# Masked self-attention on one core: rows and values turned by transposing transfers, scores of two heads and two blocks per run on 64-row tiles

## The chip, the cores and the metric

The kernel runs on one core of one Trainium2 chip. The metric is device time in microseconds (us) of the whole program, the median of several runs; beside it stands one profiled execution of the same program, with its own span.

The core's engines are named as in the profile: PE multiplies matrices (PEld is its loading of weights), ACT applies functions such as the exponential, DVE does element-wise work, POOL and SP mostly issue transfers (POOLq and SPq are their queues). SBUF is the on-chip memory of 128 rows (partitions); PSUM is the memory of 8 banks that PE writes, each 512 f32 columns wide.

## The reference, cut to what matters

```python
# x: (16, 512, 1024) f32; mask: (16, 1024) of 0 and 1; Wq, Wo: (512, 512)
xt = jnp.transpose(x, (0, 2, 1))                      # B, T, D
q = xt @ Wq.T
qh = q.reshape(B, T, 8, 64).transpose(0, 2, 1, 3)
scores = 0.125 * jnp.einsum('bhqd,bhkd->bhqk', qh, qh)
logits = (scores * cmask + (1.0 - cmask) * -1e30) * rmask
attn = jax.nn.softmax(logits, axis=-1)
ctx = jnp.einsum('bhqk,bhkd->bhqd', attn, qh)         # values are the queries
out = ctx.transpose(0, 2, 1, 3).reshape(B, T, D) @ Wo.T
return x + jnp.transpose(out, (0, 2, 1))
```

Queries, keys and values are one projection, so scores are symmetric. A token whose mask is 1 attends to all tokens whose mask is 1. A token whose mask is 0 has equal logits and gets the plain mean of all values.

## The kernel before

About half of a batch's 1024 tokens are active. For each of the 16 batches (a loop index `b`) the kernel gathers the active rows to the front, pads to a width `A` of 544 columns (5 batches), 528 (9) or 512 (2), and does the attention on these alone; the other rows get one projected mean added. Above 512 columns, the last 32 or 16 tokens are "the tail" and have their own small tiles.

The steps for a batch, by function:

- `index`, `gather`: a one-hot product finds the rows; POOL moves them in by indirect transfers, four tiles `xa` of 128 x 512 and one tail tile `xt`.
- `xt`: turns each tile on PE (four f32 transposes, L486) into columns; `xsplit` (L444, L445) copies them from PSUM as a sum of two f16 parts, `xh` on ACT and `xl` on DVE.
- `query`: `q` = Wq x, in eight accumulations (four 128-row groups `e`, each two heads; two column halves `g`) of 12 products (L513): weight high x input high, high x low, low x high.
- `qsplit`: DVE splits `q` into f16 parts; four copies on SP's queue (L540 to L543) build `xx`, which puts a head's high part on 64 rows and its low or high part on the other 64. A product over all 128 rows then gives two of the score terms at once.
- `value`: turns the queries back into rows on PE (L569) and copies them (L572); the squares' row maxima (`squares`, `peaks`, `top`, `bottom`) give the shift `nm` of each head's exponentials. `value_tail` does the same for the tail.
- `scores`: for head `p` and block `i` of 128 tokens, four products (two terms, two column halves, L701) into two of PSUM's banks, then one exponential on ACT with its row sum (L705). There are two such pairs of banks. With `i` None it does the tail tokens of four heads on 32-row outputs (L676).
- `attend`: sums over blocks, values as weights, on 64-column tiles of PE for the two heads of a pair, in f32 (L726); the tail's part on 128 rows (L730); the sums are copied by ACT (L734).
- `recip_sums`, `recip_rows`: reciprocals of the row sums, turned on PE (L764), written to memory and read back as broadcast rows `rb` (L769, L773). Four times a batch, once per pair of heads.
- `norm`: multiplies (L799), mixes in the mean for padding (L800) and splits into f16 `ch`, `cl`.
- `project`: twelve 512-wide products per 128 tokens (L817), added to the gathered row (L822) and scattered by POOL (L901). `project_tail` does the tails of three batches together. `rest` adds the mean to inactive rows (L888).

`run` lays out 18 steps a batch: one step per pair of heads and block, and two for the tails. Beside each step's two runs of scores it hands out other work of the batch before (its norms and projections) and of the next (turns, queries, values) by the planned costs in a list `m`. The final order on PE is the scheduler's, with priorities (`high_priority`) and edges (`issue_after`) where the text asks for them. A shift above `MMAX` raises a flag that lets a slow general path run after all.

Of the kernel before, what the change touches and what calls it, by code (L numbers as in the profile page):

```python
# [32 lines left out]
CQ = C + 2  # L33
# [3 lines left out]
MMAX = 60.0  # L37
# [9 lines left out]
class Fast:  # L47
# [12 lines left out]
    def __init__(self, ctx, tc, x, x_nat, mask_t, wq_t, wo_t, out):  # L60
# [9 lines left out]
        self.ps_s = pool("ps_s", 2, space=PS)  # L70
        self.ps_av = pool("ps_av", 1, space=PS)
        self.ps_m = pool("ps_m", 2, space=PS)
        self.st = {}
        self.group_first = None
# [14 lines left out]
    def pm(self, shape):  # L89
        return self.ps_m.tile(shape, F32, tag="m", name="pm")  # L90


    def setup(self, mask_t):
# [42 lines left out]
        self.qt = fixed("qt", [P, 2, HG, CT])  # L136
        self.number = iota("number", [P, B - 2], [[1, B - 2]], 2, 0)

    def setup2(self):
# [4 lines left out]
        self.xh = fixed("xh", [P, DC, CQ], F16)  # L144
        self.xl = fixed("xl", [P, DC, CQ], F16)
        for t in (self.xh, self.xl):
            nc.gpsimd.memset(t[:, :, C + 1:], 0.0)

        self.rcol = [fixed("rcol%d" % k, [P, P]) for k in range(2)]
        self.smcol = [fixed("smcol%d" % k, [P, P]) for k in range(2)]  # L150
        for t in self.rcol + self.smcol:
            nc.gpsimd.memset(t, 0.0)

        self.two = fixed("two", [P, DK], F16)
        nc.vector.tensor_tensor(self.two, self.ident[:, :DK], self.ident[:, DK:], ALU.add)
# [3 lines left out]
        self.par = fixed("par", [P, 2])  # L159
        nc.vector.tensor_tensor(self.par, self.quad[:, 0:2], self.quad[:, 2:4], ALU.add)  # L160

        self.low = fixed("low", [P, 1])
        nc.vector.tensor_reduce(self.low, self.ident.rearrange("p (r k t) -> p k r t", r=HG, k=2)[:, 1], AX.XY, ALU.add)
        self.sign = fixed("sign", [P, 1])
        nc.vector.tensor_scalar(self.sign, self.low, -2.0, 1.0, ALU.mult, ALU.add)

    def load(self, name, c, half=None, after=None):
# [4 lines left out]
        raw = self.sb([P, D], F32, "xa", 13)[:, cols]  # L172
# [3 lines left out]
    def split(self, name, c, half=None):  # L176
# [3 lines left out]
        nc.scalar.activation(hi, raw, AF.Copy, scale=SW)  # L180
# [3 lines left out]
    def order(self):  # L184
# [5 lines left out]
        for j in range(TB):  # L190
            nc.tensor.matmul(pn, lhsT=self.on16, rhs=mh[:, :, j], start=(j == 0), stop=(j == TB - 1))
        key = self.sb([P, B], F32, "sc", 3)
        nc.vector.scalar_tensor_tensor(key, pn, 32.0, self.number, ALU.mult, ALU.add)
        more = self.sb([P, B, B], F16, "c", 4)
# [7 lines left out]
        who = self.sb([P, B, B], F16, "c", 4)  # L202
# [5 lines left out]
    def permute(self):  # L208
# [3 lines left out]
        each = self.sb([P, B, TB, B], F16, "ch", 2)  # L212
# [145 lines left out]
    def warm(self, n):  # L358

        t = self.ps_av.tile([P, P], F32, tag="av", name="warm")  # L360
        with self.behind(self.pe):
            for _ in range(n):
                self.nc.tensor.matmul(t, lhsT=self.on16, rhs=self.on16, start=True, stop=True)
# [939 lines left out]
```

## Time and profile before

| | |
|---|---|
| median of 3 runs | 1043.4 us (1042.15 to 1043.84) |
| span of the profiled execution | 1032.2 us |
| PE busy | 988.2 us, 96% |
| DVE busy | 725.1 us, 70% |
| ACT busy | 659.5 us, 64% |
| moved by transfers | 177.73 MB |

The span runs from the first to the last instruction. Busy time of PE counts each product until its modelled end, and products overlap; in the timeline each row names the start, the busy length, the engine, the line of the kernel, the tiles out and in, and how many instructions the row merges. In the groups by line, `x` is the count, then follow total busy time and mean length in ns, then the idle time before them and who ended it.

### The profile page before, as it was taken

Reading aid. Unit: us, or ns where it says so; the run is one execution under the profiler, and the core shown is the slowest. Engines: PE = TensorE matmul, PEld = TensorE weight load, DVE = VectorE, ACT = ScalarE, POOL = GpSimd, SP = SyncE. Lnnn points to the kernel's source line nnn. Section 1 sums busy time; section 2 is a strip of 40 time slices with the busy share of each in tenths; the row PEclk is TensorE's granted clock in tenths of the full one; section 3 lists DMA queues with packets and bytes.
Section 4 is the critical chain, followed back from the end, with each engine's and each line's share of the span. In section 5 each row is a group of like instructions: output and inputs, shape, how many; then the busy total and the mean of one; then the engine's idle time right before and its main releaser. Section 6 shows DMA issues by size and latency. Waiting matters only on the chain. (4 is left out here: it accounts for less than half of the span.)

```text
span 1032.2 us, 23511 instructions
## 1 busy us (share of the span) xinstructions
PE 988.2 (96%) x8455; PEld 685.0 (66%) x8455; DVE 725.1 (70%) x2410; ACT 659.5 (64%) x1702; POOL 300.8 (29%) x307
## 2 busy tenths in 40 slices
PE   7798999999999999999999999999999999999996
PEld 6576667666676766767666676767666666776563
DVE  6897668676775767877666787767777777666653
ACT  5876767557667666667667567756667667665550
POOL 3101013223311232233232333323232322325562
PEclk9999999999999999999999999999999999999999
DMA  6746546557554586575657565576565666556652
GB/s 199 231 139 183 136 134 161 183 161 206 165 142 128 150 239 172 151 209 148 190 157 227 172 169 168 163 203 185 163 210 138 192 184 184 151 142 191 185 183 95
DMA packets 78795, 177.73 MB, mean 172 GB/s; under 512 B 14688, under 2 KB 20576, under 8 KB 78672
## 3 DMA queue, kind: packets, MB, share of 16 engines
q1 hardware_dynamic: 57584, 108.40, 38.8%
q0 software_dynamic: 21088, 67.75, 20.9%
q8 instruction: 69, 1.13, 0.5%
q14 instruction: 54, 0.44, 0.1%
HBM read 91.49 MB, written 33.91 MB: 121 GB/s over the span
## 5 line engine op out<-in xcount | busy, mean ns | idle before, releaser
L705 ACT ACTIVATE p<-pss,nm 128x528 f32<-128x528 f32 (+2 forms) x512 | 359.5, 706 | 169.6 <-PE pss L701 160.0
L701 PE MATMUL pss<-xx 128*128 128x264 f16 (+2 forms) x2048 | 300.9, 276 | 6.1 <-ACT p L705 5.2
L726 PE MATMUL pav<-p,v 128*64 128x264 f32 (+2 forms) x2048 | 243.3, 390 | 0.0
L701 PEld LDWEIGHTS <-xx 128*128 128x128 f16 x2048 | 194.2, 99 | 62.4 <-issue 25.1
L726 PEld LDWEIGHTS pav<-p,v 128*64 128x64 f32 x2048 | 141.4, 137 | 85.7 <-issue 13.5
L901 POOL DMA_INDIRECT y_out<-xa,idx x68 | 73.5, 1081 | 285.4 <-PE pss L701 101.6
L513 PE MATMUL pm<-xh,wqh 128*128 128x264 f16 (+5 forms) x512 | 142.2, 278 | 4.1 <-DVE xa L822 3.4
L513 PE MATMUL pm<-xl,wqh 128*128 128x264 f16 (+5 forms) x512 | 141.6, 277 | 0.2 <-DVE xl L445 0.2
L513 PE MATMUL pm<-xh,wql 128*128 128x264 f16 (+5 forms) x512 | 141.7, 277 | 0.0
L395 POOL DMA_INDIRECT xa<-x_in,idx x68 | 68.6, 1009 | 201.7 <-PE pss L701 81.1
L513 PEld LDWEIGHTS <-wqh 128*128 128x128 f16 x1024 | 98.3, 99 | 24.0 <-issue 7.5
L705 ACT ACTIVATION_READ_ACCUMULATOR p<-pss,nm 128x1 f32 x512 | 103.9, 203 | 0.0
L901 POOL DMA_INDIRECT y_out<-xi,idx x60 | 72.6, 1211 | 97.0 <-PE pss L701 26.5
L817 PE MATMUL pm<-woh,ch 128*128 128x512 f16 x240 | 91.1, 379 | 0.0
L817 PE MATMUL pm<-woh,cl 128*128 128x512 f16 x240 | 90.9, 379 | 0.0
L817 PE MATMUL pm<-wol,ch 128*128 128x512 f16 x240 | 90.9, 379 | 0.0
L395 POOL DMA_INDIRECT xi<-x_in,idx x60 | 61.3, 1021 | 95.3 <-PE pss L701 31.9
L516 ACT ACTIVATE q<-pm 128x264 f32<-128x264 f32 (+5 forms) x128 | 50.2, 392 | 59.9 <-PE pm L513 59.3
L822 DVE SCALAR_TENSOR_TENSOR xa<-pm,xa 128x512 f32<-128x512 f32 x60 | 41.3, 689 | 56.4 <-PE pm L817 52.7
L817 PEld LDWEIGHTS <-ch 128*128 128x128 f16 x480 | 46.1, 98 | 44.8 <-issue 0.9
L799 DVE TENSOR_TENSOR c<-c,rb 128x528 f32<-128x528 f32 (+2 forms) x64 | 45.4, 710 | 43.0 <-DMA rb<-rd 21.3
L888 DVE TENSOR_TENSOR xi<-xi,ub 128x512 f32<-128x512 f32 (+1 forms) x60 | 40.8, 688 | 41.8 <-PE pss L701 41.2
(223 smaller groups left out, 1509.6 us busy)
## 6 DMA issues: line engine op xcount, KB each, us to landing
xx<-hl SPq DMA_DIRECT2D x224, 136.0 KB
xm<-x_nat_in SPq DMA_DIRECT2D x56, 512.0 KB
rb<-rd SPq DMA_DIRECT2D x72, 132.0 KB
rb<-rd SPq DMA_DIRECT2D x40, 136.0 KB
pt<-c SPq DMA_DIRECT2D x36, 132.0 KB
pt<-p SPq DMA_DIRECT2D x36, 132.0 KB
ub<-ud SPq DMA_DIRECT2D x16, 256.0 KB
xx<-hl SPq DMA_DIRECT2D x32, 128.0 KB
```

The costliest lines, as they stand in the source:

```text
L395: dma = self.nc.gpsimd.indirect_dma_start(out=tile[:n], out_offset=None, in_=self.x, in_offset=bass.IndirectOffsetOnAxis(ap=idx, axis=0))
L513: self.beat = nc.tensor.matmul(pq, lhsT=w[:, c, e * P:(e + 1) * P], rhs=xx[:, c, cols], start=(k == 0), stop=(k == 3 * DC - 1)).ins
L516: nc.scalar.activation(s["q"][:, e, cols], pq, AF.Copy, scale=1.0 / (SX * SW))
L701: self.beat = nc.tensor.matmul(pt[:, g, :CH], lhsT=xx[:, 2 * k, i * P:(i + 1) * P], rhs=xx[:, 2 * k + a, g * CH:(g + 1) * CH], start=(a == ...
L705: self.exp = [nc.scalar.activation(t.rearrange("p (g c) -> p g c", g=2), pt[:, :, :CH], AF.Exp, bias=s["nm"][p // HG][:, p % HG:p % HG + 1 ...
L726: mm = nc.tensor.matmul(s["pav"][k * DK:(k + 1) * DK, g, :CH], lhsT=s["v"][p][:, i, k * DK:(k + 1) * DK], rhs=ps[k][:, cols], start=(i == ...
L799: self.once(nc.vector.tensor_tensor(c[:, :A], c[:, :A], s["rb"][p], ALU.mult), self.beat if p < 3 else None)
L817: nc.tensor.matmul(po[:cols.stop - cols.start], lhsT=a[:, e, cols], rhs=w[:, e, :], start=(e == 0 and k == 0), stop=(e == DC - 1 and k == 2))
L822: self.nc.vector.scalar_tensor_tensor(x, po, 1.0 / (SX * SW), x, ALU.mult, ALU.add)
L888: self.once(self.nc.vector.tensor_tensor(x[:n], x[:n], s["ub"][:n], ALU.add), self.beat)
L901: dma = self.nc.gpsimd.indirect_dma_start(out=self.out, out_offset=bass.IndirectOffsetOnAxis(ap=idx, axis=0), in_=x, in_offset=None)
```

## The change

- `xt` (from the second batch on): ACT and DVE scale and split the gathered rows while they are still rows, and a transposing transfer on SP's queue writes the turned f16 parts into `X`. No product and no PSUM.
- `query`: the copy from PSUM writes the two f16 parts at once (`hl`). The copies into `xx` are gone.
- `value` (from the second batch on): two transposing transfers turn the two f16 parts; `value_sum` adds them on DVE, later in the order.
- `scores`: a run is a head pair and two blocks. One head's products use the upper 64 rows of PE and the other's the lower 64, three terms each, into one tile `S` of five banks. Where the width is not 512, two narrow strips that would share a bank are computed on all 128 rows from masked columns `edge`. Four exponentials follow. Eight runs a batch.
- `attend` works per head pair after its blocks are done, each column half in a bank of the shared pool (three banks); the tail's part is f16.
- `recip_sums`, `recip_rows`, `peaks`, `top`, `bottom` run once a batch, not per pair or half.
- Each product on PE is tied to the one before (`then`), so PE keeps the order of the text, which eight lists `fill` in `run` lay out.

Core of the diff:

```diff
+        self.S = self.ps_s.tile([P, 5 * 512], F32, tag="s", name="pss")
...
+    def then(self, i):
+        if self.last_pe is not None:
+            self.tc.add_manual_dep(i.ins, self.last_pe.name,
+                                   mybir.DependencyInfo(mybir.DependencyClass.NoSync, mybir.DependencyReason.DATA),
+                                   reason="products keep the order of the text")
+        self.last_pe = self.pe = i.ins
+        return i
...
     def xt(self, b, k):
...
+                hs = s["hs"][:n, k:k + 1]
+                t = self.sb([P, 2, D], F16, "xs", 2)
+                with self.behind(*self.exp):
+                    nc.scalar.activation(t[:n, 0], x[:n], AF.Copy, scale=hs)
+                nc.vector.scalar_tensor_tensor(t[:n, 1], x[:n], hs, t[:n, 0], ALU.mult, ALU.subtract)
+                nc.sync.dma_start(out=self.X[:, :, k * P:k * P + n], in_=t[:n].rearrange("p k d -> p (k d)"), transpose=True)
...
     def query(self, b, e, g):
-        nc.scalar.activation(s["q"][:, e, cols], pq, AF.Copy, scale=1.0 / (SX * SW))
+        with self.hurry():
+            nc.scalar.activation(hl[:, 0, cols], pq, AF.Copy, scale=1.0 / (SX * SW))
+            nc.vector.scalar_tensor_tensor(hl[:, 1, cols], pq, 1.0 / (SX * SW), hl[:, 0, cols], ALU.mult, ALU.subtract)
...
     def value(self, b, e):
+            t = self.sb([P, 2, 4, P], F16, "v16", 2)
+            for k in range(2):
+                nc.sync.dma_start(out=t[:, k], in_=hl[:, k, :512], transpose=True)
...
+    def value_sum(self, b, e):
+        with self.behind(*self.exp):
+            self.once(self.nc.vector.tensor_tensor(v, t[:, 0], t[:, 1], ALU.add), self.beat)
+            self.squares(b, e)
...
+    def scores(self, b, p, half):
+        terms = (0, 0), (0, 1), (1, 0)
+        block = lambda k: slice((2 * half + k) * P, (2 * half + k + 1) * P)
+        for h in range(2 if n else 0):
+            o = 1024 if h == 0 else 1536 - n
+            for m, (t, u) in enumerate(terms):
+                self.mm(self.S[:, o:o + n], lhsT=hl[:, t, block(1 - h)], rhs=s["edge"][p][:, h, u, :], start=(m == 0), stop=(m == 2))
+        first = [(0, 0, 512), (1, 0, 512 - n // 2)] + ([(0, 512, A)] if n else [])
+        for k, x, y in first:
+            for m, (t, u) in enumerate(terms):
+                for h, (j, lo, hi) in enumerate(((k, x, y), (1 - k, A - y, A - x))):
+                    o = start[j, h]
+                    self.beat = self.mm(self.S[:, o + lo:o + hi], lhsT=hl[rows[h], t, block(j)], rhs=hl[rows[h], u, lo:hi],
+                                        start=(m == 0), stop=(m == 2)).ins
+        for k in range(2):
+            for h in range(2):
+                self.exp = [nc.scalar.activation(t, self.S[:, o:o + A], AF.Exp, bias=s["nm"][:, 2 * p + h:2 * p + h + 1], scale=SCALE,
+                                                 accum_out=s["z"][:, 2 * p + h, i:i + 1]).ins]
...
+    def attend(self, b, p):
+        for g in range(2):
+            po = self.pm([P, CH])
+            for i in range(4):
+                for k in range(2):
+                    self.mm(po[k * DK:(k + 1) * DK], lhsT=s["v"][p][:, i, k * DK:(k + 1) * DK], rhs=s["ps"][p, i, k][:, cols],
+                            start=(i == 0), stop=(i == 3 and not nt))
+            if nt:
+                self.mm(po, lhsT=s["vt"][:n, p], rhs=s["pt"][:n, p, cols], start=False, stop=(nt != CT))
...
     def run(self, flag):
+            if b:
+                fill[0] += [L(self.recip_rows, o, ALL), L(self.attend, o, 3)]
+                fill[1] += [L(self.norm, o, 0)]
...
+            for p in range(3):
+                fill[2 * p + 2].insert(0, L(self.attend, b, p))
...
+                    fill[0] += [Q(n, 0, 0)]
+                    fill[1] += [Q(n, 0, 1), V(0), Q(n, 1, 0), Q(n, 1, 1), V(1)]
+                    fill[2] += [W(0)]
+                    fill[3] += [W(1), Q(n, 2, 0), Q(n, 2, 1), V(2), Q(n, 3, 0)]
+                    fill[4] += [Q(n, 3, 1), V(3), W(2)]
+                    fill[5] += [W(3)]
...
+                fill[6] += [L(self.xt, a, 0), L(self.xt, a, 1)]
+                fill[7] += [L(self.xt, a, k) for k in (2, 3, 4)]
...
+            for st in range(8):
+                self.scores(b, st // 2, st % 2)
+                self.issue()
+                for f in fill[st]:
+                    f()
+                    self.issue()
```

In `run`, `o` is the batch before, `n` the next, `a` the one after; `Q` is `query`, `V` `value`, `W` `value_sum`. `MMAX` goes from 60 to 18, and 15 ln 2 is added to every shift (`LIFT`), which keeps the f16 tail weights in range.

More of the change, by code (lines that the diff above doesn't have):

```diff
@@ L143, in setup2 @@
         nc.vector.tensor_reduce(self.quad, self.ident.rearrange("p (r t) -> p r t", r=HG), AX.X, ALU.add)
[L144 to L151, printed above, removed]
+        self.X = fixed("X", [P, 2 * DC, CX], F16)
@@ L157, in setup2 @@
         self.big = fixed("big", [P, self.B + 2 * DC])
[L159 to L165, printed above, removed]
+        self.half = fixed("half", [P, 2])
@@ L358, in warm @@
     def warm(self, n):
[L360 to L363, printed above, removed]
+        t = self.pm([P, P])
+        for _ in range(n):
+            self.mm(t, lhsT=self.on16, rhs=self.on16)
     def post(self, transfer, before=None, urgent=True):
```

841 lines of the change are left out of this document (406 added, 435 removed).

## The prediction

> **What bounds the kernel now.** I read the spans first, then the busy shares, then the groups of lines by shape, then the product engine's timeline, and last the exponentials and the transfer queue.
>
> ```profile
> core 0: 1032.2 us, clock 0.995
> PE 988.2 (96%) x8455; PEld 685.0 (66%) x8455; DVE 725.1 (70%) x2410; ACT 659.5 (64%) x1702; POOL 300.8 (29%) x307
> ```
>
> The profiled execution took 1032.2 us between first and last instruction; the median of the runs is 1043.4, so 11.2 us lie around the span. PE is covered for 96%, at full granted clock. Busy time counts a product until its modelled end, so what one costs is read from start to start in the timeline:
>
> ```profile
> 516.27 0.38 PE L817 MATMUL pm<-woh,ch 128*128 128x512 f16 x1
> 516.48 0.38 PE L817 MATMUL pm<-wol,ch 128*128 128x512 f16 x1
> 516.70 0.38 PE L817 MATMUL pm<-woh,cl 128*128 128x512 f16 x1
> 517.01 0.63 PE L676 MATMUL pss<-xx 128*32 128x264 f16 x16
> 517.57 0.33 PE L628 MATMUL pm<-ident,smcol 128*128 128x128 f32 x1
> 518.19 0.28 PE L513 MATMUL pm<-xh,wqh 128*128 128x264 f16 x1
> 518.30 0.28 PE L513 MATMUL pm<-xl,wqh 128*128 128x264 f16 x1
> 518.41 0.28 PE L513 MATMUL pm<-xh,wql 128*128 128x264 f16 x1
> ...
> 520.67 3.78 PE L726 MATMUL pav<-p,v 128*64 128x264 f32 x32
> 524.38 0.62 PE L701 MATMUL pss<-xx 128*128 128x264 f16 x4
> ```
>
> Listed at 0.38 us, a 512-wide f16 product takes 0.2155 from start to start; one of 264 takes 0.112. That is 0.42 ns a column: PE streams without gaps, and columns are what a product costs. Two more readings. Sixteen products on 32-column tiles take 517.57 - 517.01 = 0.56 us, 35 ns each: four run side by side. And entering that tiling took 517.01 - 516.70 = 0.31 instead of 0.215, so a change of tiling costs about 0.094 us. The groups by shape give what there is to save:
>
> ```profile
> L701 PE MATMUL pss<-xx 128*128 128x264 f16 x1152 | 168.3, 276 | 1.5 <-ACT p L705 1.0
> L701 PE MATMUL pss<-xx 128*128 128x272 f16 x640 | 96.6, 279 | 2.4 <-ACT p L705 2.2
> L701 PE MATMUL pss<-xx 128*128 128x256 f16 x256 | 36.3, 272 | 2.2 <-ACT p L705 2.0
> L486 PE MATMUL pm<-ident,xa 128*128 128x128 f32 x240 | 33.0, 277 | 0.0
> L569 PE MATMUL pm<-two,xx 128*128 128x64 f16 x480 | 24.9, 193 | 1.6 <-DMA xx<-hl 1.3
> L764 PE MATMUL pm<-ident,rcol 128*128 128x128 f32 x64 | 18.9, 296 | 2.0 <-DVE rcol L758 1.8 <-DVE xl L445 0.2
> ```
>
> PE hardly waits for anyone (the last column), so time taken off PE comes off the span, unless something else steps in.
>
> **The change part by part, on PE.**
>
> Scores. Before, 2048 products of mean width 265.5 (L701): 2048 x 0.1127 = 231 us. After, a run covers two heads and two blocks, 128 runs in all, with three terms instead of four half-width ones, and each product is 64 rows deep, paired with one of the other head on the other 64 rows. A term has 1024 columns a tile at every width (512 + 496 + 16, 512 + 480 + 32, 512 + 512). If a pair runs side by side, a run is 3 x 2 x 0.2155 = 1.29 us: 165 us. The 336 pairs that are 16 or 32 wide cost no less than the 9-wide products of the next fence (8 in 511.62 - 511.42 = 0.20, 25 ns): +6. The 672 products for the edges, on all 128 rows: 17. Sum 188, gain 43.
>
> ```profile
> 511.42 0.35 PE L325 MATMUL pm<-oht,tmp 128*128 128x9 f16 x8
> 511.62 0.95 PE L701 MATMUL pss<-xx 128*128 128x264 f16 x7
> ...
> 528.07 0.41 PE L569 MATMUL pm<-two,xx 128*128 128x64 f16 x8
> 528.32 1.06 PE L701 MATMUL pss<-xx 128*128 128x264 f16 x8
> ...
> 532.92 1.04 PE L486 MATMUL pm<-ident,xa 128*128 128x128 f32 x8
> 533.80 0.61 PE L701 MATMUL pss<-xx 128*128 128x264 f16 x4
> ```
>
> No product here is 64 rows deep, so the pair must be bounded: 0.2155 if the tiles run together, 0.431 if one after the other (165 us more). The nearest rows are the column tiles, L676 and L726, which do run together; I take 0.2155.
>
>
> Changes of tiling. Counted in the two instruction lists, the tiling of consecutive products changes 197 times before and 488 times after (into and out of every run of scores, and around each small tail product inside a head pair's sums). 291 x 0.094 = 27 us lost. The bound below is 24 less, if row tiles need no drain at 256 of them.
>
> Turning the rows. 240 products of L486 (0.88/8 = 0.11 us) and some 50 for tails (about 0.09) leave PE: gain 31. Turning the values: 480 x 0.031 (0.25/8): gain 15. Small turns: L764 from 64 to 17, the other maxima and tails likewise, all at about 0.11: gain 13. The tail scores fall from 28 runs of 0.56 to 9 of about 0.66 and 5 of 1.37, and the tail sums become f16: gain 8. Queries, output products and the f32 sums over blocks keep their columns.
>
> Sum: 43 - 27 + 31 + 15 + 13 + 8 = 83 us less on PE.
>
> **What hides the rest.** ACT: eight half-width copies replace four wide ones, four squarings a batch replace one, and the copies of values and tails go. The scores now have one set of banks: a run's first product waits for all four exponentials of the run before.
>
> ```profile
> L425 ACT ACTIVATE xm<-xm 128x1024 f32<-128x1024 f32 x56 | 58.9, 1052 | 0.0
> L552 ACT ACTIVATE tmp<-v 128x512 f32<-128x512 f32 x17 | 10.9, 640 | 0.1
> L445 DVE SCALAR_TENSOR_TENSOR xl<-pm,xh 128x512 f16<-128x512 f32 x60 | 38.8, 683 | 11.8 <-ACT xh L444 11.5
> L516 ACT ACTIVATE q<-pm 128x264 f32<-128x264 f32 x36 | 14.0, 389 | 14.2 <-PE pm L513 13.8
> ...
> 529.55 0.71 ACT L705 ACTIVATE p<-pss,nm 128x528 f32<-128x528 f32 x1
> 530.14 0.21 ACT L705 ACTIVATION_READ_ACCUMULATOR p<-pss,nm 128x1 f32 x1
> 530.24 0.71 ACT L705 ACTIVATE p<-pss,nm 128x528 f32<-128x528 f32 x1
> ```
>
> The first four rows price ACT's and DVE's other pieces below: a sum of the input 1.05 (and 0.2 for reading its sum), a squaring or scaling of 512 columns 0.64, a difference 0.68, a half-width copy 0.39. Back to back the exponentials are 0.69 apart (the read of the sum overlaps). So the loop is run 1.42 + 0.3 (a product's modelled 0.28, and hand-over) + 4 x 0.69 + 0.39 for a copy of the sums that stands between them = 4.9 us. PE's own work in the shortest of a batch's eight stages is 1.42 + 3.71 (L726 above: both halves of a head pair) = 5.1; the others have 5.5 to 7.5. The waits are just covered in the middle of the kernel. They are not at its ends: two stages of the first batch carry 0.5 and 1.6 us of other products, two of the last none. (4.9 - 1.9) + (4.9 - 3.0) + 2 x (4.9 - 1.4) = 12 us, which I add.
>
> DVE loses the casts and differences of the queries, the copies for the second operand and three quarters of the reciprocal chains, and gains the differences from PSUM, the value sums and the edges; below its 725 us, off the path. One wait is new there: the value sums wait for a turned transfer, with norms and query differences queued behind them, and PE's three banks for queries wait for those. They stand a stage (5 us) after the issue.
>
> Transfers. 256 copies of the split queries go; 13 transposing transfers a batch come, on SP's queue with everything else there.
>
> ```profile
> 511.39 0.35 SPq L769 DMA_DIRECT2D rd<-rr  x1
> 512.69 1.09 SPq L773 DMA_DIRECT2D rb<-rd  x2
> ...
> xa<-x_in,idx POOLq DMA_INDIRECT x68, 5.4
> ```
>
> A transposing transfer has no row. Below: 0.55 us of queue and 1.3 us to land, like the small copies (rb waits for rd). Above: 5.4 us, which an indirect move of as many bytes (256 KB) takes to land, and the queue held for as long. The cover: the last three turns of a batch can start about 5.9 us into the last stage (1.42 + 0.3 + 2.76, then a scaling of 0.65 and a difference of 0.7), and PE reaches the first query after the rest of that stage (two output products, 5.2) and a run, a head pair and the tail scores, at about 13 us. So 7 us cover three turns: any price up to 5.4 is hidden if they overlap each other; if they queue at 5.4 each it isn't. Nearest, in queue and in kind, are the direct copies, and I cost it at nothing.
>
> The Trainium skill ("Advanced Engine Details and Errata", X-Bar Transpose) calls transposing transfers as fast as regular ones, by which they cost nothing here; its "DMA: Bandwidth & Descriptors" (DGE: Hardware vs Software) rates the hardware generator, the one used, worse at transposes, which leans to the queue's rival below. No run here shows either.
>
> Span: 1032.2 - 83 + 12 = 961; time 961 + 11 = 972.
>
> **The rivals.**
>
> *Row tiles one after the other* (the other side). Each run pays 1.29 us again: 972 + 165 = 1137. For it: no row shows a 64-row product, and both tiles read the same two streams of one tensor. Against: column tiles do overlap, and the pair writes different banks. It decides from 0.2155 + 71/768 = 0.31 us a pair (768 pairs of 512 columns), where the gain is gone.
>
> *Row tiles overlap in part.* At 0.28 us a pair, about a third of the way up, 768 x 0.065 = 50 us come back: 1022. For it: each tile's weights are loaded anew for each product, two loads to a pair. Against: the four column tiles of L676 reload too, and four cost 0.14 for 264 columns, little above the 0.112 of one. The Trainium skill ("TensorE: Matmul & The Clock Gate", Part 3) measured 3.07 times from four row tiles, not four, which would put a pair at about this price; the trace has no row tile to compare.
>
> *Turned transfers hold SP's queue.*
>
> ```profile
> L701 PEld LDWEIGHTS <-xx x2048: 95/98/181, 33.0 to 1007.7; 128*128 128x128 f16 x187
> ```
>
> At 5.4 us for 256 KB and 2.7 for the 128 KB of values, a batch needs 4 x 5.4 + 1 + 8 x 2.7 = 44 us, and some 36 copies at 0.55 add 20: 64 us on SP. PE needs 56: the scores now start at 33.0 and end at 1007.7, 61 us a batch, less 83/16. Then the queue sets the pace, reciprocals and first queries come late: 972 + 14 x 8 = 1084, slower too. It decides where a large turn takes over 5 us of the queue. For it: they share one queue, and the reciprocals' copies stand right behind the last row turns. Against: SP's copies cost a tenth of that.
>
> *ACT's loop shows.* Row sums of the input (1.25 us each), squarings and scalings stand behind the fourth exponential, 2.3 to 2.7 us in five stages, against 1.7 of the next run. Each delays the next run by 0.5 to 1 us where PE has only 5.1 to 5.5 to do: about 2 us a batch, 972 + 30 = 1000. For it: PE keeps the order of the text and can't take a later product. Against: most stages are longer on PE.
>
> *The change doesn't do what it says.* The guard on the largest shift falls from 60 to 18; above it the slow general path would run. From the reference's inputs the largest shift is 16.7, so it doesn't.
>
> **How the numbers follow.** Forecast 0.54; ACT's loop 0.13; row tiles in part 0.07; queue 0.15; row tiles in sequence 0.09; another 0.02. The forecast's own range is 915 (no drain, shorter stalls than now) to 1000. All together 915 to 1090, which leaves out row tiles in sequence and the worse half of the queue. About 0.2%, 2 us, is what this kernel's measurement can tell. Faster 0.74 (the first three), slower 0.24 (the queue and the sequence), same 0.02.
>
> **What would show it.** Right: starts of the 512-wide score products in pairs a few ns apart, 0.215 us from pair to pair; PE's span near 960, with waits for ACT only in the first and last batch; 0.09 us at each change of tiling. Wrong: pairs at 0.43; queries or value sums idle behind a DMA for microseconds; SP's transposing issues of several us each; PE idle before most runs of scores, released by ACT.

## The result and the profile after

The changed kernel takes 1141.97 us (median of 4 runs, 1129.7 to 1148.1) against 1043.27 for the kernel before: a ratio of 1.091, with a 95% interval of 1.085 to 1.097. One of these four runs, and below one each of one_rb and both_late_again, took over 1.5% longer than the fastest of its kernel and counts as slow: it is in the median but not in the ratio, and one_rb's trace is of such a run. The forecast was 972, in a range up to 1090. The first lines of the profile's page, its transfers and the group of value sums:

```profile
span 1143.1 us, 22661 instructions
...
PE 969.2 (85%) x8363; PEld 562.2 (49%) x8363; DVE 642.9 (56%) x1951; ACT 638.5 (56%) x1660; POOL 307.8 (27%) x304
...
DMA packets 195801, 166.80 MB, mean 146 GB/s; under 512 B 149922, under 2 KB 158948, under 8 KB 195684
...
L590 DVE TENSOR_TENSOR v<-v 128x512 f32<-128x512 f16 x60 | 41.3, 689 | 143.2 <-DMA v<-hl 102.4
```

```profile
core 0: 1143.1 us, clock 0.939
```

PE has less to do (969 us busy, 988 before), yet stands still for 1143.1 - 969.2 = 174 us, where it stood for 44. Its clock was granted at 0.939: 2 x (1 - 0.939) x 1143.1 = 139 us at half speed, against 10. Value sums on DVE stand 102 us for turned transfers. And less bytes move in 2.5 times as many packets.

The busy time by stage, cut at the first and the last exponential; each row has start and end, the length, busy time of PE, PEld, DVE, ACT and POOL, the granted clock, the transfers' share and GB/s. Before:

```profile
0.00:34.00 34.00, 26.17 (x272) 22.24 (x273) 22.82 (x90) 19.52 (x50) 10.53 (x31) 0.95 0.69 207
34.00:1008.00 974.00, 947.23 (x8104) 656.02 (x8103) 693.67 (x2300) 638.28 (x1649) 284.47 (x270) 1.00 0.61 173
1008.00:1032.20 24.20, 14.76 (x82) 6.78 (x80) 8.66 (x22) 1.69 (x5) 5.77 (x6) 0.93 0.25 92
```

After:

```profile
0.00:54.20 54.20, 37.09 (x341) 29.04 (x342) 31.95 (x131) 22.08 (x50) 12.21 (x32) 0.82 0.50 159
54.20:1113.10 1058.90, 913.53 (x7929) 525.38 (x7930) 598.05 (x1788) 615.14 (x1607) 289.63 (x266) 0.94 0.57 147
1113.10:1143.10 30.00, 18.56 (x96) 7.77 (x94) 12.89 (x32) 1.28 (x4) 5.98 (x6) 0.95 0.25 91
```

The head costs 20 us more, the end 6, and the batches between them 85: most of the loss comes back every batch. There PE's busy time fell by 34 while its idle time rose from 27 to 145.

PE's own work went nearly as forecast. The strips at the edges, a run of scores and the next product in the timeline after:

```profile
570.05 0.30 PE L103 MATMUL pss<-edge,hl 128*128 128x32 f16 x6
570.29 1.51 PE L103 MATMUL pss<-hl 64*128 64x512 f16 x18
571.73 0.39 PE L103 MATMUL pm<-woh,ch 128*128 128x512 f16 x1
```

Edges 0.24 us, the run 571.73 - 570.29 = 1.44; inside it the two products of a pair start 3 to 4 ns apart and pairs follow each other after 0.21. The 64-row tiles run side by side.

What PE, DVE and ACT wait for (line, releaser: total, number, longest):

```profile
DVE v L590 <- DMA v<-hl: 102.4, 15, 10.1
...
ACT xs L526 <- DMA X<-xs: 52.8, 25, 5.5
...
PE pss L103 <- ACT p L727: 42.7, 21, 3.7
...
ACT p L727 <- remote: 33.4, 5, 9.9
...
PE pm L106 <- DVE smcol L645: 18.9, 9, 4.2
...
PE pm L103 <- DVE hl L558: 17.2, 11, 2.3
```

"Remote" is a wait for which the profile shows no releaser. Two things stand out that the forecast had set to nothing: landings of turned transfers, and exponentials that start late for no visible reason. The first, in SP's queue at the end of one batch:

```profile
584.93 14.06 SPq L528 DMA_TRANSPOSE X<-xs  x5
599.09 0.42 SPq L819 DMA_DIRECT2D rd<-rr  x1
600.84 0.51 SPq L825 DMA_DIRECT2D rb<-rd  x1
...
610.98 0.59 SPq L828 DMA_DIRECT2D rb<-rd  x1
611.68 1.19 SPq L763 DMA_DIRECT2D pt<-th  x2
...
619.50 0.59 SPq L765 DMA_DIRECT2D pt<-th  x1
620.19 5.16 SPq L579 DMA_TRANSPOSE v<-hl  x4
```

The merged row of 14.06 us holds five turns and the stands between them:

```profile
L528 SPq DMA_TRANSPOSE X<-xs x5: 1144/1232/2207, 584.9 to 597.8; - x5
```

Their own issues take 1.14 to 2.21 us (shortest, middle and longest in ns), 7.1 together. In the other 7 us SP stands for rows that ACT and DVE have yet to scale, and since the queue is in order all that is behind stands too. Behind them and `rd` stand sixteen copies of `rb` and twelve of `pt`, and only then, at 620.19, the values' first turns. DVE at the same place:

```profile
608.68 0.71 DVE L851 TENSOR_TENSOR c<-c,rb 128x528 f32<-128x528 f32 x1 [5.13 <-remote]
...
611.15 0.43 DVE L558 SCALAR_TENSOR_TENSOR hl<-pm,hl 128x266 f16<-128x266 f32 x1
...
612.94 0.41 DVE L558 SCALAR_TENSOR_TENSOR hl<-pm,hl 128x266 f16<-128x266 f32 x1
...
624.12 0.69 DVE L590 TENSOR_TENSOR v<-v 128x512 f32<-128x512 f16 x1 [6.43 <-DMA v<-hl]
```

And ACT, in the stage before:

```profile
592.07 0.72 ACT L526 ACTIVATE xs<-xa,hs 128x512 f16<-128x512 f32 x1 [1.55 <-DMA X<-xs]
...
596.33 0.72 ACT L526 ACTIVATE xs<-xt,hs 16x512 f16<-16x512 f32 x1 [3.44 <-DMA X<-xs]
596.96 0.68 ACT L727 ACTIVATE p<-pss,nm 128x528 f32<-128x528 f32 x1
```

The queries of the first two values were split at 611.6 and 613.4, themselves held up by a start 5 us late without a releaser (608.68); their turns start 8.6 and 9.5 us after that (620.19, 622.82), and DVE stands 6.43 us at the head of its order. On ACT the last two scalings wait 1.55 and 3.44 us for an earlier turn to leave one of two `xs` buffers: the second and third turn were issued at 586.25 and 591.37, so they gave their buffers back 5.8 and 5.0 us later. The exponentials whose scores were done at 593.9 stand behind the last scaling.

### The profile page after: what moved, and what is told of

The parts are those of the page before. It is cut to its first block, busy times and chain, and to the rows that moved or that the text cites. A ratio compares the mean times of both kernels' runs of the same rounds, so it can differ in the third digit from the quotient of the medians.

```text
span 1143.1 us, 22661 instructions
## 1 busy us (share of the span) xinstructions
PE 969.2 (85%) x8363; PEld 562.2 (49%) x8363; DVE 642.9 (56%) x1951; ACT 638.5 (56%) x1660; POOL 307.8 (27%) x304
## 2 busy tenths in 40 slices
DMA packets 195801, 166.80 MB, mean 146 GB/s; under 512 B 149922, under 2 KB 158948, under 8 KB 195684
## 4 chain that ended last, share of the span: by engine, by line
PE 55%; DMA 12%; ACT 10%; DVE 9%; issue 7%; SPq 5%; another core or an unknown queue 2%; POOL 0%; POOLq 0%; DVEq 0%; ACTq 0%
PE pm L103 39%; PE pss L103 15%; ACT p L727 6%; DMA X<-xs 5%; DMA v<-hl 3%; DVE xi L939 1%; SPq L825 1%; SPq L763 1%; DMA rb<-rd 1%; SPq L828 1%; ACT xs L526 1%; DVE v L590 1%; DMA pt<-th 1%; DVE top L481 1%
## 5 line engine op out<-in xcount | busy, mean ns | idle before, releaser
L103 PE MATMUL pm<-p,v 128*64 128x264 f32 (+2 forms) x2048 | 273.0, 409 | 9.8 <-issue 8.7
L103 PE MATMUL pss<-hl 64*128 64x512 f16 (+4 forms) x2208 | 214.6, 336 | 6.6 <-ACT p L727 5.9
L103 PE MATMUL pm<-X,wqh 128*128 128x264 f16 (+5 forms) x1024 | 189.0, 286 | 25.6 <-DVE sc L335 12.6
L103 PEld LDWEIGHTS <-hl 64*128 64x128 f16 (+1 forms) x2912 | 131.2, 99 | 157.6 <-issue 73.6
L103 PEld LDWEIGHTS pm<-p,v 128*64 128x64 f32 x2048 | 143.2, 142 | 96.6 <-issue 25.3
L103 PE MATMUL pm<-X,wql 128*128 128x264 f16 (+5 forms) x512 | 146.2, 286 | 2.2 <-issue 2.2
L590 DVE TENSOR_TENSOR v<-v 128x512 f32<-128x512 f16 x60 | 41.3, 689 | 143.2 <-DMA v<-hl 102.4
L952 POOL DMA_INDIRECT y_out<-xi,idx x60 | 79.3, 1322 | 49.0 <-DVE xi L939 33.4
L785 ACT COPY c<-pm 128x264 f32<-128x264 f32 (+2 forms) x128 | 47.9, 380 | 77.5 <-PE pm L103 59.8
L557 ACT ACTIVATE hl<-pm 128x264 f16<-128x264 f32 (+5 forms) x128 | 50.2, 404 | 44.9 <-PE pm L103 37.2
```

Of the source, the lines that this page charges most:

```text
L103: return self.then(self.nc.tensor.matmul(out, lhsT=lhsT, rhs=rhs, start=start, stop=stop))
L557: nc.scalar.activation(hl[:, 0, cols], pq, AF.Copy, scale=1.0 / (SX * SW))
L590: self.once(self.nc.vector.tensor_tensor(v, t[:, 0], t[:, 1], ALU.add), self.beat)
L785: nc.scalar.copy(c[:, cols], po)
L952: dma = self.nc.gpsimd.indirect_dma_start(out=self.out, out_offset=bass.IndirectOffsetOnAxis(ap=idx, axis=0), in_=x, in_offset=None)
```

## The experiments

One theory was that the transposing transfers cost the time, by their place in one queue and by who stands for them. Its rivals: the fixed order on PE with one set of score banks (PE stops for every late exponential), the order alone, the transposition itself, and, from the traces of the first runs, exponentials released late while POOL issues indirect transfers. The runs went to several chips. Each ratio is against the kernel before on the same chip, where it takes 1032.7 us in one group (free_order, before_in_order, score_halves, both_late) and 1039.9 to 1043.8 in all others.

### One transfer back to PE at a time

rows_pe turns the rows on PE in every batch as in the first; values_pe does so with the values, right after each query; both_pe does both.

```diff
@@ xt (rows_pe, both_pe); value (values_pe, both_pe)
-        if b == 0:
+        if True:
@@ xt
-                pt = self.S[:, k * 512:k * 512 + DC * n].rearrange("p (c n) -> p c n", c=DC)
+                pt = self.S[...] if b == 0 else self.pm([P, DC, n])
```

> Rows are turned on TensorE again in every batch (62 blocks, four turns of about 0.11 us each: 28 us more of PE); values still come by transposing transfers. Theory A (the row turns hold SP's queue for about 3 us each at the batch's end, ACT's scalings wait for their landing, and the reciprocals' copies, the copies of the tails' weights and the value turns stand behind them): the time falls although PE gets more to do, by 5 us in each of 15 batches less 28/15, to 1060 to 1110. Rival B (one set of score banks and the fixed order of products set the pace): slower by the 28 us, 1150 to 1170. Rival C (the value turns alone are the delay): about 1140 to 1170, with the value sums' wait for DMA (102 us now) unchanged.

> Values are turned on TensorE again in every batch (480 products of 128 columns more, about 0.056 us each: 27 us of PE, and 60 copies of 0.64 us on ACT: 38 us); rows still come by transposing transfers. Theory A (both kinds of turn cost, the value turns through the value sums that stand on DVE for 102 us): 1060 to 1110. Rival B (score banks and order): 1170 or more. Rival C (the value turns alone): 1000 to 1040.

> No transposing transfer at all: rows and values are turned on TensorE (55 us more of PE than the changed kernel). Theory A: the forecast's 972 plus 55, so 1015 to 1045, with PE busy for 93% or more. Rival B (score banks and order set the pace): 1150 or more, PE as idle as now.

Measured: rows_pe 1134.75 us, ratio 1.0896 [1.0855, 1.0937], no gain over the changed kernel, as none of its theories expected; values_pe 1206.71, 1.156 [1.154, 1.158]; both_pe 1198.96, 1.152 [1.147, 1.157]. The last two are worse for a reason of their own. PE's waits in both_pe:

```profile
PE pm L103 <- ACT hl L557: 55.1, 59, 5.8
...
PE pm L103 <- DVE hl L558: 21.4, 68, 1.5
```

With the order fixed, PE stands right after each query for the copy and the difference that make its two parts, 77 us in all. So they don't tell what the transfers cost; the next group turns the values later.

### The turns on PE, but late

both_late has no turned transfer after the first batch either, and turns the values where the changed kernel adds them (`value_sum`), a stage after the query. values_late does this for the values alone, and values_late_xs4 also gives `xs` four buffers (the changed kernel has no room for them). late_free is both_late without the fixed order.

```diff
@@ value
-            t = self.sb([P, 2, 4, P], F16, "v16", 2)
-            for k in range(2):
-                nc.sync.dma_start(out=t[:, k], in_=hl[:, k, :512], transpose=True)
@@ value_sum
+        pv = self.pm([P, 4, P])
+        for k in range(4):
+            for t in range(2):
+                self.mm(pv[:, k, :], lhsT=hl[:, t, k * P:(k + 1) * P], rhs=self.id16, start=(t == 0), stop=(t == 1))
         with self.behind(*self.exp):
-            self.once(self.nc.vector.tensor_tensor(v, t[:, 0], t[:, 1], ALU.add), self.beat)
+            nc.scalar.copy(v, pv)
             self.squares(b, e)
@@ xt (values_late_xs4)
-                t = self.sb([P, 2, D], F16, "xs", 2)
+                t = self.sb([P, 2, D], F16, "xs", 4)
@@ then (late_free)
-        if self.last_pe is not None:
+        if False:
```

> No transposing transfer, as both_pe, but the values are turned on TensorE where the changed kernel has the value sums, one stage later, so that PE doesn't stand for the query's copy and difference (76 us of both_pe's waits). Theory A (the transfers are the delay): 1015 to 1060. Theories O and S: both_pe's 1199 less about 80, 1105 to 1140, no better than the changed kernel, which has 55 us less for PE to do.

> As both_late, but rows come by transposing transfers as in the changed kernel; values are turned on TensorE a stage after their queries. PE has 27 us more to do than the changed kernel. Theory V (the value turns, through the value sums that DVE stands for, are the larger cost, and the row turns cost what rows_pe gave back, some 35 us): 1055 to 1085. Theory R (row turns are the larger cost): 1110 or more.

> values_late with four buffers instead of two for the scaled rows, so that ACT's next scaling doesn't wait for an earlier row turn to land. If that wait is how the row turns cost: 10 to 30 us under values_late. If it is the issue on SP's queue and the landing ahead of the first query: within 8 us of values_late.

> both_late with the products left to the scheduler instead of the order of the text. Theory O on top of A (the order costs the first batch some 12 us, and a few us elsewhere): 1025 to 1045, level with the kernel before or under it. If the order costs nothing once the transfers are gone: 1045 to 1060.

Measured: both_late 1052.56 us, 1.021 [1.017, 1.025]; values_late 1138.11, 1.092 [1.090, 1.094]; values_late_xs4 1123.97, 1.077 [1.071, 1.083]; late_free 1136.30, 1.089 [1.085, 1.093]. In its own group both_late lies 64 us under free_order (below) and 84 under score_halves, which have all the transfers: without them PE is 93% busy. Neither is the changed kernel itself, which was not run there: one has a free order, the other, as shown below, longer runs of scores (0.27 us in each of 128, some 35 us). Two more `xs` buffers are worth 1138 - 1124 = 14 us; ACT's stand for the row turns, 55.8 us in values_late, all but goes (0.7). But late_free, which has none of the transfers, was no better than the changed kernel, on another chip. That had to be the order or the chip.

### The order, the banks, the copies, the transposition

free_order lifts the fixed order from the changed kernel; before_in_order puts it on the kernel before; score_halves orders a run's products so that a block's exponentials can start at half of it; one_rb joins the sixteen `rb` copies of a batch to two; plain_copies moves the same bytes over the same queue unturned, but for the tails of 16 or 32 rows; its rows and values are left unturned.

```diff
@@ free_order: then
-        if self.last_pe is not None:
+        if False:
@@ before_in_order: every matmul and transpose of the kernel before
-        self.nc.tensor.matmul(
+        self.mm(
@@ score_halves: scores
+        edges(1)
+        for m in range(3):
+            part(0, 0, 0, 512, m)
+            part(1, 0, n, A, m)
...
+        edges(0)
+        for m in range(3):
+            part(0, 1, 0, A - n, m)
+            part(1, 1, w, A, m)
@@ one_rb: recip_rows, for k in range(2)
+            nc.sync.dma_start(out=rb[rows, p0:p1, :512], in_=heads.unsqueeze(0).broadcast_to([DK, p1 - p0, 512]))
@@ plain_copies: value (xt likewise)
-                nc.sync.dma_start(out=t[:, k], in_=hl[:, k, :512], transpose=True)
+                nc.sync.dma_start(out=t[:, k], in_=hl[:, k, :512].rearrange("p (c n) -> p c n", n=P))
```

> The changed kernel with the products left to the scheduler again (no dependency from each product to the one written before it); all else as changed. Theory O (PE stands at the head of its list for what isn't ready, with ready products behind it, and each stand also halves the clock for 3.4 us): the first exponential comes at about 40 us instead of 54, PE's time in waits falls by half, and the time to 1030 to 1080. Theory S (the single set of score banks and ACT's loop pace it): 1110 to 1140. Theory A (transposing transfers): 1110 to 1150 as well, since nothing about them changes; rows_pe and both_pe speak against it already.

> The kernel before with one addition: every product is tied to the one written before it, so PE runs them in the order of the text (no other part of the change). Theory O: 40 to 100 us slower than before, 1085 to 1145, with the granted clock under 0.97. Theories S and A: within 1% of before, 1035 to 1055.

> The changed kernel with the products of a run of scores in another order: first all of block 0 of both heads, then all of block 1, so that the next run can start when the first two exponentials are done and the first two exponentials when half of the run is. Same products, same pairs of row tiles, same sums. Theory S (ACT's loop with one set of banks): PE's waits for the exponentials (43 us now) fall under 15 us, and the time to 1085 to 1115. Theory O: the waits move to the next thing in the list, 1120 to 1145.

> The reciprocals are spread by two to four transfers a batch instead of eight to sixteen (same bytes; one buffer for all four pairs instead of four single ones). SP's queue is shorter by about 12 x 0.64 = 8 us at each batch's start; the value turns are issued that much earlier. Theory A, in the form that small copies between the row turns and the value turns are what the value sums wait for: the wait of the value sums falls from 102 us to under 40 and the time by 5 us a batch, to 1050 to 1090. If only the row turns' landing counts: within 15 us of the changed kernel's 1142.

> The changed kernel with every full transposing transfer replaced by a plain copy of the same bytes between the same tiles at the same place in SP's queue: rows and values arrive unturned, so the output is other than the reference's (the turns are left out), and the count of failed guards is multiplied by zero so that the fast path ends alone. If it is the transposition that makes these transfers slow to issue and to land: 1000 to 1080. If it is their place in an in-order queue, behind and ahead of the small copies: 1120 to 1145.

Measured: free_order 1116.65 us, 1.082 [1.078, 1.087]; before_in_order 1131.83, 1.097 [1.092, 1.102]; score_halves 1136.22, 1.100 [1.095, 1.104]; one_rb 1137.33, 1.088 [1.084, 1.092]; plain_copies 1120.90, 1.075 [1.073, 1.076].

- A fixed order alone makes the kernel before 9.7% slower, but its text was not written to be kept. In the changed text the order is no such price: with the transfers gone, late_free and the fixed order (1.0906, both_late_again below) agree within their intervals, on two chips.
- Unturned copies save about 17 us of the 99. By itself that can't tell turning from place: on the same chip late_free, with no such transfer at all, is no faster. The waits tell more. A copy of rows is issued in 0.62 us instead of 1.28 and one of values in 0.49 instead of 1.22 (medians), yet most of the stands remain (102.4 and 52.8 us in the changed kernel):

```profile
DVE v L590 <- DMA v<-hl: 87.2, 13, 9.3
...
ACT xs L526 <- DMA X<-xs: 35.5, 16, 3.3
```

- The Trainium skill ("Advanced Engine Details and Errata", X-Bar Transpose) calls turned transfers as fast as regular ones; here their issue took twice as long. The table that rates the hardware generator worse at transposes (DGE: Hardware vs Software), which the prediction places on another page, stands on that one too.
- score_halves and one_rb don't decide: the first stretched a run from 1.69 us (the median with edges and changes of tiling) to 1.96 and still shows 39.6 us of waits for exponentials; the second cut the value sums' waits to 57 us, with no gain beyond the noise.

```profile
PE pss L103 <- ACT p L740: 39.6, 18, 3.9
```

```profile
DVE v L590 <- DMA v<-hl: 57.3, 18, 7.6
```

### The same kernels on another chip

late_head is both_late with the fixed order only after the first batch's head. The other three are kernels already seen, once more, on one chip.

```diff
@@ late_head: then
-        if self.last_pe is not None:
+        if self.last_pe is not None and self.paced:
```

> The changed kernel itself, beside both_late on one chip. The runs so far were made on three chips; on the one that both_late, free_order, score_halves and before_in_order had, the kernel before takes 1033 instead of 1043 us, and no exponential there starts more than 0.5 us after the product that it waits for, while on the other two some 20 to 25 do, by 50 to 66 us together. Theory A (transfers): both_late stays 60 to 120 us ahead of this one on whichever chip. Theory C (the chip's late wake-ups are what the changed kernel pays, the transfers little): on the chip with 1043 us both_late is within 30 us of this one; on the chip with 1033 us this one comes down to 1060 to 1090.

> both_late on the same chip as the changed kernel. Theory A: ratio to before 1.01 to 1.04 again, wherever it runs. Theory C: 1.02 where before takes 1033 us, 1.07 to 1.10 where it takes 1043 us.

> both_late with the order of the text enforced from the first batch's stages on only; the products before them are the scheduler's. The first exponential of both_late comes at 46 us against 34 before, so 6 to 12 us less than both_late, if the order is what delays the head; within 3 us of both_late if not.

> The kernel before, for its profile on the same chip: if exponentials that start late after their products are the chip's doing, they are in this trace too where it takes 1043 us, with little cost, since the scheduler's order has other products for PE to run.

Measured: after_again 1138.14 us, 1.093 [1.088, 1.098]; both_late_again 1139.51, 1.091 [1.088, 1.093]; late_head 1144.52, 1.095 [1.091, 1.099]; before_again 1049.1 in one run, span 1047.4. The same both_late took 1052.56 on one chip and 1139.51 on another, 87 us apart, while the kernel before differs by 11. That is as theory C had it, and not theory A. late_head gains nothing: its first exponential comes at 53.1 us, against 54.0 in both_late_again. The two traces of both_late hold the same products in the same order, and the second falls behind in steps. One such step, first where it is missing:

```profile
556.56 1.51 PE L103 MATMUL pss<-hl 64*128 64x512 f16 x18
556.56 0.99 POOL L421 DMA_INDIRECT xi<-x_in,idx  x1 [0.30 <-issue]
...
558.11 0.71 DVE L842 TENSOR_TENSOR c<-c,rb 128x528 f32<-128x528 f32 x1 [0.19 <-PE pss L103]
...
558.17 0.70 ACT L718 ACTIVATE p<-pss,nm 128x528 f32<-128x528 f32 x1 [1.26 <-PE pss L103]
```

In both_late_again:

```profile
606.64 1.51 PE L103 MATMUL pss<-hl 64*128 64x512 f16 x18
606.64 0.99 POOL L421 DMA_INDIRECT xi<-x_in,idx  x1 [0.30 <-issue]
...
610.46 0.91 POOL L421 DMA_INDIRECT xi<-x_in,idx  x1 [0.30 <-issue]
...
613.03 0.71 DVE L842 TENSOR_TENSOR c<-c,rb 128x528 f32<-128x528 f32 x1 [5.03 <-remote]
613.09 0.70 ACT L718 ACTIVATE p<-pss,nm 128x528 f32<-128x528 f32 x1 [6.10 <-remote]
```

The run of scores lasts as long in both. In the first the exponential starts 0.1 us after its end; in the second ACT and DVE start 4.9 us after it, when POOL's row of four gathers (606.64, 607.93, 609.21, 610.46) has ended. PE itself goes on meanwhile, and the trace's record of semaphore updates shows that its signals come late: the product that ends the run at 608.15 and two later ones that end at 609.61 and 610.96 are told at 613.01, 613.13 and 613.26, in one bunch. In both_late the same three are told as they end (558.09, 559.55, 560.90). The start at 608.68 in the changed kernel is of the same kind: products that end at 603.70 and 605.16 are told at 608.65 and 608.78. I counted the exponentials in each trace that start over 0.5 us after both their last score product and ACT's work before them. both_late has none, and so have free_order and score_halves on that chip; both_late_again has 27, 67 us together, after 19 (54 us), after_again 19 (55 us), at nearly the same places. Take the exponentials that had to wait for their scores, and the indirect transfers that POOL issues from 2 us before the end of these to 1 us after. With two or more, 27 of 42 are late in both_late_again and 18 of 32 in after_again; with one, 0 of 30 and 0 of 33; with none, 0 of 51 and 0 of 36. But in both_late, on the other chip, 0 of 43 are late with two or more, and in before_again, on the same chip, 0 of 53: such issues alone don't make a start late. By the profile's own account of waits (both_late_again, then before_again, on the same chip), exponentials without a visible releaser waited 49.4 us against 2.4:

```profile
ACT p L718 <- remote: 49.4, 10, 9.9
```

```profile
ACT p L705 <- remote: 2.4, 1, 2.4
```

### Indirect transfers one to a run

spaced_gathers lets POOL issue at most one indirect transfer per run of products, from the second batch on; late_spaced does the same to both_late.

```diff
@@ issue
-        if line:
+        if line and (self.beat is not self.beat_used or not self.paced or not self.batch):
+            self.beat_used = self.beat
```

> The changed kernel with GpSimd's indirect transfers spread out: from the second batch on, at most one of them is issued for each run of products (each waits for its own product instead of four or five for the same one). Same transfers, same order of products. In the traces so far 17 to 25 exponentials a run start 0.5 to 7.6 us after the end of the product they wait for, and nearly all of them at places where GpSimd issues two or more indirect transfers back to back; where it issues none, not one of about 40 does. Theory G (back-to-back indirect transfers hold up the product engine's signals, and the changed kernel, with one set of score banks and one order, stands still for it): where before takes 1043 us, under 8 such late starts and 1060 to 1105 instead of 1139. Theory N (a coincidence of place: the batch's start is slow for another reason): as many late starts, 1130 to 1150. Where before takes 1033 us there are no late starts to remove and nothing is told by this run alone.

> both_late (no transposing transfer) with the indirect transfers spread out in the same way. Theory G: from both_late_again's 1139 to 1050 to 1090 where before takes 1043 us, as both_late had 1053 on the chip without late starts. Theory N: 1130 to 1150.

Measured: spaced_gathers 1137.66 us, 1.091 [1.086, 1.095]; late_spaced 1087.11, 1.043 [1.039, 1.048]. Late starts fall to 3 (2.9 us) and 9 (9.0 us). With the turned transfers in place it gains nothing, though the late starts are gone as theory G expected. Value sums wait longer instead, in spaced_gathers:

```profile
DVE v L591 <- DMA v<-hl: 146.4, 23, 12.7
```

Without them it gains 1139.5 - 1087.1 = 52 us (on two chips; by the ratios to the kernel before, 49). And with gathers spread, taking the turned transfers away gains 1137.7 - 1087.1 = 51, though PE then has the turns to do again. Each of the two hides the other: alone, neither removal shows on these chips, both together give about 50.

No version beats the kernel before. What is left of late_spaced's 4%, against before_again's phases: the first exponential comes at 55.4 instead of 36.5, and 48.7 us instead of 23.7 lie behind the last one, 15 of them in one stand of PE at the end, which both spaced kernels have and both_late has not (1.7 us there):

```profile
PE pss L103 <- DVE ch L846: 15.1, 1, 15.1
```

## Why the prediction was wrong, step by step

**"I cost it at nothing" (the transposing transfers): the step that failed.** I asked whether three turns fit into 7 us of cover, a question of how long a turn takes. What cost was the order, and an overlap that was not there: "hidden if they overlap each other" left out that the scaled rows have two `xs` buffers. In the batch shown two row turns held theirs for 5.0 and 5.8 us, near the upper bound, and five turns took SP 14 us where their own issues add up to 7. A value turn stands behind 28 small copies; a value sum, at the head of DVE's order, stands for its landing with whatever DVE does next behind it; a scaling at the head of ACT's order stands for a buffer that a turn still reads, with exponentials behind it. The queue's rival named the queue, but priced it by capacity, with a point of decision ("over 5 us of the queue") that was not reached: no turn took over 2.5 us of the queue, most 1.2 to 1.3. The runs show the price: 51 us with the gathers spread (spaced_gathers against late_spaced, one chip), and some 64 in both_late's group (against free_order, which has another order of products). How it divides between turning and place is read from the traces and plain_copies' waits, not shown by a time.

**A wait that the prediction did not have.** With one set of score banks, PE's next run stops for every late exponential. On the chips where before takes 1040 to 1044, exponentials start up to 7.6 us late while POOL issues indirect transfers in a row; that is worth about 50 us where the turned transfers are gone. The kernel before shows hardly any such wait (4 late starts, 6.5 us in before_again). A free order alone doesn't ride over it: late_free has 25 late starts, 64 us together, and is no faster. That two sets of banks would is argued, not shown. Why PE's signals are late, and why not on one chip or in the kernel before, stays open; the changed kernel itself was not run on that chip.

**"Below its 725 us, off the path" (DVE): wrong.** It is less busy, 643, but its order is on the path: query differences and row maxima (`smcol`) come late, and PE waits for them (17.2 and 18.9 us).

**The clock was not priced.** PE's busy time holds work at half speed. A stretch of the changed kernel's trace, cut at the clock's own steps, columns as in the table by stage:

```profile
345.10:348.50 3.40, 0.60 (x6) 0.12 (x2) 1.35 (x5) 1.81 (x6) 2.69 (x3) 1.00 0.92 267
348.50:351.90 3.40, 1.70 (x8) 0.76 (x10) 0.00 (x0) 0.88 (x2) 0.08 (x1) 0.50 0.95 237
351.90:355.30 3.40, 3.40 (x16) 1.36 (x12) 0.00 (x0) 0.56 (x2) 0.00 (x0) 0.50 0.51 109
355.30:358.70 3.40, 3.40 (x40) 2.35 (x40) 1.60 (x3) 1.57 (x5) 0.00 (x0) 1.00 0.50 104
```

After 3.4 us in which PE was busy for 0.60 us, the next 3.4 run at half clock; they are half busy, and the next 3.4 run at half clock too; those are full, and the clock is back. The Trainium skill ("TensorE: Matmul & The Clock Gate", Part 1: The HAM clock gate) gives this window of 3.4 us and calls it idle; here a window need not be idle: in this trace each window at full clock in which PE was busy for under 42% was followed by half clock (but for the first, in which the program starts), and none above 56% was. PE is busy in 118 of the 139 us at half clock, against 7 of 10 before, and work that takes twice as long there adds (118 - 7) / 2 = 56 us, an estimate from these traces. So a stall costs more than its length.

**PE's sum (83 us less): nearly right.** 969 less 59 (118 / 2) is 910 at full clock, against 988 less 3: 75 us less. The row tiles run side by side, as taken from the column tiles, and neither rival on them came true. score_halves agrees with 0.094 us a change of tiling: two more and strips that lost their partner cost 1.96 - 1.69 = 0.27.

**The sum's other terms.** "Around the span" I put 11.2 us; in the runs of this study 1.7 to 2.1 lie there (1144.93 against 1143.1). The rest belongs to an execution quicker than the median, not to the kernel; whether that was another chip the record doesn't say. For the ends I added 12; head and end cost 26. ACT's loop was to be covered in the middle; PE waits 42.7 us for exponentials in all. In both_late, without turns and late releases, it waits 13.8, so the rival on ACT's loop (some 30 us) was near in size, but most of that wait seems to have other causes.

In sum, from the span of 1032.2: -75 for work, +56 for the clock and +130 for standing still give the 111 us more.

## What to carry to other kernels

Ask of a transfer on an in-order queue not only how long it takes but what stands ahead of it, and ask of the instruction that consumes it what stands behind that: an engine at 56% can still set the time. When PE has one set of score banks, every late exponential reaches it, and a stall can halve its clock for the next 3.4 us, sometimes for 7 or more. Remove two suspects together as well as one at a time; here each hid the other.

## What the runs showed of the hardware

- Two 64-row tiles of PE share the array fully: the second product of a pair starts 3 to 4 ns behind the first, and 512 columns of both take 0.21 us.
- The issue of a turned transfer of 256 KB takes SP 1.28 us (median of 60, at most 2.2), one of 128 KB 1.22; unturned, 0.62 and 0.49. Packets under 512 bytes are 149,922 with the turned ones, 85,602 where plain copies stand in their place, 19,842 without them (both_late) and 14,688 in the kernel before.
- On most of the chips, engines that wait for PE in the changed kernel and its variants start up to 7.6 us late while POOL issues indirect transfers 1.3 us apart; in the step shown, PE's signals come in a bunch, 2.3 to 4.9 us late. On one chip no exponential of three variants was late, and the kernel before has hardly any late start.
- In the changed kernel's trace each window of 3.4 us at full clock with PE busy for under 42% is followed by half clock (but for the first), and none above 56% is.
